# Cross-attention on one core: which engine issues the first two moves of a quad's probabilities, and what SyncE issues ahead of the slot's loads

## The chip, the core and the metric

The kernel runs on one core of one Trainium2 chip. The metric is the device time of one execution in microseconds; the median of 3 runs before is 567.95 us (567.91 to 568.03). Short names of the engines, as the profile has them: PE is TensorE (PEld its weight loads), DVE is VectorE, ACT is ScalarE, POOL is GpSimd, SP is SyncE. SPq and ACTq are the queues from which SyncE and ScalarE issue DMAs.

## The reference

Layer norm of x, a query projection, attention of 32 heads of width 32 over a context that is both keys and values, an output projection and a residual:

```python
# x, ctx_4096: (8, 256, 1024) float32; the mask is all ones; Wq, Wout: (1024, 1024)
mu = jnp.mean(hidden_states, axis=-1, keepdims=True)
var = jnp.var(hidden_states, axis=-1, keepdims=True)
x = (hidden_states - mu) * jax.lax.rsqrt(var + LN_EPS) * ln_gamma + ln_beta
Q = _split_heads(x @ Wq.T)
K = _split_heads(memory_keys)
V = _split_heads(memory_values)
scores = jnp.einsum('bhsd,bhtd->bhst', Q, K) * scale
scores = jnp.where(mask, scores, -jnp.inf)
probs = jax.nn.softmax(scores, axis=-1)
attn = jnp.einsum('bhst,bhtd->bhsd', probs, V)
attn = attn.transpose(0, 2, 1, 3).reshape(B, S, HIDDEN)
out = attn @ Wout.T
return residual + out
```

## The kernel before

All data is float32. The work is cut into 64 quads: quad n is four heads (index j, 0 to 3) of batch n // 8, so eight quads make a batch. An outer loop over slots, n = 0 to 63, writes every engine's instructions in a fixed order by hand (`tc.manual_schedule()`); engines run their own streams in order and meet at semaphores. Slot n holds, on PE, the scores of quad n + 1 (`scores`, L486), the product of probabilities and values of quad n - 2 (`values`, L636), and pieces of the query projection of a later batch (L447) and of the output projection of the batch before (L720). From batch 2 on, both projections go by a scheme of seven half-size products; weights for it are kept in DRAM and read back through a tile `ring` (L412).

`softmax_parts(n)` writes the softmax of one quad. For each head and each half of the 256 queries DVE adds the mask bias and takes the row minimum of the negated scores (L524, with a read of its accumulator, `mn`), and ACT takes the exponential and its row sum (L528, `den`). DVE inverts the sums (L535, `rden`), POOL multiplies (L543; in some quads DVE or ACT does a head), and DVE transposes 32 x 32 blocks of each head into a tile `pT` (`blocks`, L549). The scores lie in four PSUM buffers, one per head, that the next quad's scores overwrite: PE can start the next scores only when DVE has read these.

A 32 x 32 block transpose does not carry blocks across partitions. The rest is done by moving quarters of 32 partitions. `pT` has two halves (index 0 and 1) on the second dimension. ACT copies aside the second half into a tile `pc` (`aside`, L555), two heads at a time, the second time behind the last block transpose. Then `tail` issues four DMAs of 128 KB each:

- the first two moves (L614): first half of partition group 2r + 1 to the second half of group 2r, for r = 0 and 1; they overwrite what `aside` read, so they wait for it;
- the second two moves (L618): from `pc`, group 2r, to the first half of group 2r + 1; they overwrite what the first moves read, so each waits for a first move's landing.

Between the first two and the second two SP issues the loads of the slot (`between`): keys for quads n + 4 and n + 5 (L135, `load_k`) or values for two later quads (L143, `load_v`), and in some slots residual rows `r` (L149), half of a later x (L129), a mask, halves of `ring` (L412). Loads in `ahead` stand ahead of all four moves. After the tail, in some slots, ACT normalizes half of an x (L248), DVE takes its statistics (L227) or transposes it (L316), SP issues four or six moves of x (`move_x`, L332), and results are sent out (L763).

For quads 0 to 7 and 57 to 63 the tail is put off into the next quad's softmax (`tails`); for quads 8 to 56 it stands at the end of the quad's own softmax. There the next thing on ACT behind the second copy aside is, but for a normalization of x in some slots, the next quad's first exponential. Tiles rotate: three buffers for `pT` and for `pc`, two for keys and for values, four for `r`.

Of the kernel before, what the change touches and what calls it, by code (L numbers as in the profile page):

```python
# [59 lines left out]
def xattn_kernel(  # L60
# [10 lines left out]
    nc = tc.nc  # L71
# [4 lines left out]
    NQ = NC  # L76
# [4 lines left out]
    K = 32  # L81
# [4 lines left out]
    N = B * NQ  # L86
# [404 lines left out]
    def softmax(*args):  # L491
        for _ in softmax_parts(*args):
            pass
# [2 lines left out]
    BY_ACT = range(1, 2 * NQ)  # L496
    BY_DVE = range(NQ, 2 * NQ)


    def softmax_parts(n, copies=(), ahead=(), between=(), hooks={}, fill=()):  # L500

        fill = list(fill)

        def fill_in():
            if fill:
                fill.pop(0)()  # L510

        pss = scs[n]
        pT = pTs[n] = ptp.tile([P, 2, NI, NH, NS, K], F32, tag="pT", name=f"pT_{n}")
        pc = asp.tile([P, NI, NH, NS, K], F32, tag="pc", name=f"pc_{n}")
        es, mns, dens = {}, {}, {}

        def exps(j, part=range(NS)):
            if 0 in part:
                es[j] = ep.tile([P, NS, T], F32, tag="e", name=f"e_{n}_{j}")
                mns[j] = sm.tile([P, NS], F32, tag="mn", name=f"mn_{n}_{j}")  # L520
                dens[j] = sm.tile([P, NS], F32, tag="den", name=f"den_{n}_{j}")
            e, mn, den = es[j], mns[j], dens[j]
            for s in part:
                nc.vector.tensor_tensor_reduce(  # L524
                    out=e[:, s, :], in0=pss[j][:, s, :], in1=mbs[n // NQ], scale=1.0,
                    scalar=NO_SCORE, op0=ALU.add, op1=ALU.min, accum_out=mn[:, s : s + 1],
                )
                nc.scalar.activation(  # L528
                    e[:, s, :], e[:, s, :], AF.Exp, bias=mn[:, s : s + 1], scale=-1.0,
                    accum_out=den[:, s : s + 1],  # L530
                )

        def normalize(j):
            rden = sm.tile([P, NS], F32, tag="rden", name=f"rden_{n}_{j}")
            nc.vector.reciprocal(rden, dens[j])  # L535
            for s in range(NS):
                if j == NH - 1 and n in BY_ACT:
                    nc.scalar.activation(
                        es[j][:, s, :], es[j][:, s, :], AF.Copy, scale=rden[:, s : s + 1]
                    )  # L540
                    continue
                engine = nc.vector if j == 1 and n in BY_DVE else nc.gpsimd
                engine.tensor_scalar(  # L543
                    es[j][:, s, :], es[j][:, s, :], rden[:, s : s + 1], 1.0,
                    ALU.mult, ALU.mult,
                )

        def blocks(j):
            nc.vector.transpose(  # L549
                pT[:, :, :, j, :, :].rearrange("p a i s k -> p (a i) s k"),  # L550
                es[j].rearrange("p s (b t) -> p b s t", t=K),
            )

        def aside(j):
            nc.scalar.copy(pc[:, :, ts(j, 2)], pT[:, 1, :, ts(j, 2)])  # L555

        if n == 0:
            for j in range(NH - 1):
                exps(j, (0,))
            yield  # L560
            exps(NH - 1, (0,))
            fill_in()
            yield
            for j in range(NH):
                exps(j, (1,))
            normalize(0)
            fill_in()
        else:
            exps(0)
            while tails:  # L570
                tails.pop()()
            for done in list(pvs):
                copy_at(done)
            exps(1)
            for hook in hooks.get("soon", ()):
                hook()
            exps(2)
            normalize(0)
            exps(3)
        if n <= NQ + 1:  # L580
            for copy in copies:
                copy()
        for hook in hooks.get(0, ()):
            hook()
        normalize(1)
        fill_in()
        if n in BY_DVE:
            normalize(2)
        blocks(0)
        for hook in hooks.get(1, ()):  # L590
            hook()
        if n not in BY_DVE:
            normalize(2)
        fill_in()
        if n in BY_ACT:
            normalize(3)
        blocks(1)
        aside(0)
        if n not in BY_ACT:
            normalize(3)  # L600
        fill_in()
        blocks(2)
        while fill:
            fill_in()
        if n > NQ + 1:
            for copy in copies:
                copy()

        def tail():
            blocks(3)  # L610
            aside(1)

            for r in range(2):
                nc.sync.dma_start(pT[ts(2 * r, K), 1], pT[ts(2 * r + 1, K), 0])  # L614
            for load in between:
                load()
            for r in range(2):
                nc.sync.dma_start(pT[ts(2 * r + 1, K), 0], pc[ts(2 * r, K)])  # L618

        for load in ahead:  # L620
            load()
        if n < NQ or n > N - NQ:
            tails.append(tail)
        else:
            tail()
        yield
# [16 lines left out]
    def copy_at(n):  # L643
        b, c = divmod(n, NQ)
        k, c = divmod(c, NK)
        if c == 0:
            ats[b, k] = atp.tile([P, NK, NS, NA, K], F32, tag="at", name=f"at_{b}_{k}")
        for r, pv in enumerate(pvs.pop(n)):
            nc.scalar.copy(
                ats[b, k][:, c, :, ts(r, 2), :], pv.rearrange("p a s k -> p s a k")  # L650
            )
# [245 lines left out]
    for c in range(NC):  # L897
        copy_x0(1, c, nc.scalar if c < NC // 2 else nc.vector)
    first = softmax_parts(0, (partial(copy_q, 1), partial(copy_q, 2)), (), (), {}, [
        partial(ln_stats, 1, 0), partial(ln_stats, 1, 1),  # L900
        partial(ln_norm, 1, 0, nc.vector),
# [17 lines left out]
    for b in range(B - 1):  # L919
        done, ends = 0, b == B - 2  # L920
        for i, counts in enumerate(steps_of(b)):
            n = NQ * (b + 1) + i
# [15 lines left out]
    for n in range(N):  # L938
        b, i = divmod(n - NQ, NQ)
        new_q = new_qs[n]  # L940
        between = []
# [5 lines left out]
        if n + 3 in firsts or n + 2 in firsts:  # L947
            between, ahead = between + ahead, []
# [214 lines left out]
```

## Time and profile before

| | |
|---|---|
| median of 3 runs | 567.95 us (567.91 to 568.03) |
| profiled execution, from its first to its last instruction (span) | 566.0 us |
| what lies around the span, against the median | 1.95 us |
| PE, DVE, ACT, POOL busy | 561.4, 467.6, 423.4, 394.3 us |
| granted clock of PE over the span | 1.000 |
| bytes moved by DMA, mean rate | 119.02 MB, 210 GB/s |

No time of the profiled execution other than its span is given, so the span stands for it. Busy times are sums over the span; matmuls are pipelined and their ends are modelled. A row of a group reads: line, engine, operation, tile written, tile read, shapes, count, then busy us and mean ns. A row of the timeline reads: start in us, duration in us, engine, line, operation, tiles, count, and in brackets the idle time of the engine before it and what ended it. A row of waits reads: engine, line and what it waited for, then us in total, times, longest us. A row of one line's instructions reads: minimum, median and maximum duration in ns, and when the first and the last start.

### The profile page before, as it was taken

How to read it: one execution, taken by the hardware profiler on the slowest of the kernel's cores; microseconds unless marked ns; L12 is line 12 of the kernel's file. 1: busy time of each engine (PE TensorE's matmuls, PEld its weight loads, DVE VectorE, ACT ScalarE, POOL GpSimd, SP SyncE). 2: the span in 40 equal slices, each digit the busy share in tenths (PEclk: the TensorE clock that was granted, in tenths of full speed). 3: DMA queues.
4: the chain of work that ended last, by engine and by line, in shares of the span. 5: the costliest groups of instructions: out<-in, count | busy, mean ns of one | idle time of the engine just before them, and what ended most of it. 6: DMA issues, size and time to landing. Idle time of an engine off the chain costs nothing.

```text
span 566.0 us, 20200 instructions
## 1 busy us (share of the span) xinstructions
PE 561.4 (99%) x7266; PEld 393.7 (70%) x7266; DVE 467.6 (83%) x1716; ACT 423.4 (75%) x1464; POOL 394.3 (70%) x636
## 2 busy tenths in 40 slices
PE   8999999999999999999999999999999999999997
PEld 8788886767766767667766776667766767755454
DVE  5889889999988988878898888988888777879923
ACT  4699999997778866786777876778776776769820
POOL 2788887899777656857568665777648657448780
PEclk9999999999999999999999999999999999999999
DMA  8966667856697777966778767796658864536751
GB/s 310 397 181 199 185 198 228 281 162 179 212 301 232 223 202 235 263 195 191 233 216 239 215 176 221 230 273 193 176 140 269 255 191 128 146 110 180 218 156 74
DMA packets 47219, 119.02 MB, mean 210 GB/s; under 512 B 8976, under 2 KB 9744, under 8 KB 47120
## 3 DMA queue, kind: packets, MB, share of 16 engines
q1 hardware_dynamic: 46976, 117.74, 69.5%
q8 instruction: 57, 0.93, 0.8%
q14 instruction: 42, 0.34, 0.2%
q10 hardware_dynamic: 144, 0.01, 0.0%
HBM read 66.33 MB, written 11.53 MB: 138 GB/s over the span
## 4 chain that ended last, share of the span: by engine, by line
PE 97%; DMA 1%; DVE 0%; POOL 0%; ACT 0%; issue 0%; SPq 0%; POOLq 0%
PE po_S L720 21%; PE pq_A L447 19%; PE pv L636 12%; PE sc L486 12%; PE po_A L720 11%; PE pq L345 9%; PE pq_S L447 8%; PE po_end L787 3%; PE po_last L787 1%; DMA x<-in_x_dram 1%; PE po_end_s L787 0%; POOL x L885 0%; PE pq L290 0%; PE px L307 0%; ACT e L528 0%; PE px L273 0%
## 5 line engine op out<-in xcount | busy, mean ns | idle before, releaser
L543 POOL TENSOR_SCALAR e<-e,rden 128x256 f32<-128x256 f32 x466 | 215.4, 479 | 125.5 <-DVE rden L535 123.0
L528 ACT ACTIVATE e<-e,mn 128x256 f32<-128x256 f32 x512 | 254.0, 502 | 46.1 <-DVE mn L524 44.9
L549 DVE STREAM_TRANSPOSE pT<-e 128x512 f32<-128x512 f32 x256 | 178.9, 703 | 35.6 <-POOL e L543 27.5
L524 DVE CUSTOM_DVE_ANT_0 e<-sc,mb 128x256 f32<-128x256 f32 x512 | 185.3, 415 | 25.4 <-PE sc L486 25.1
L555 ACT COPY pc<-pT 128x512 f32<-128x512 f32 x128 | 79.0, 617 | 55.7 <-DVE pT L549 35.6
L528 ACT ACTIVATION_READ_ACCUMULATOR e<-e,mn 128x1 f32 x512 | 98.4, 192 | 0.0
L486 PEld LDWEIGHTS sc<-k,qa 32*128 32x128 f32 x1024 | 46.1, 184 | 42.2 <-issue 21.6
L720 PE MATMUL po_S<-wo,at 128*128 128x512 f32 x152 | 74.3, 606 | 0.0
L636 PE MATMUL pv<-pT,v 64*32 64x128 f32 x4096 | 74.1, 274 | 0.0
L486 PE MATMUL sc<-k,qa 32*128 32x256 f32 x1024 | 73.6, 401 | 0.1
L636 PEld LDWEIGHTS pv<-pT,v 64*32 64x32 f32 x4096 | 57.0, 105 | 22.5 <-issue 11.8
L720 PE MATMUL po_A<-wo,at 128*128 128x512 f32 x128 | 59.4, 605 | 0.0
L345 PE MATMUL pq<-xnT,wq 128*128 128x256 f32 (+1 forms) x240 | 55.0, 384 | 0.0
L447 PEld LDWEIGHTS pq_A<-xnT,wq 128*128 128x128 f32 x416 | 48.5, 192 | 6.2 <-issue 4.8
L345 PEld LDWEIGHTS pq<-xnT,wq 128*128 128x128 f32 x240 | 44.6, 190 | 8.2 <-issue 1.5
L720 PE MATMUL po_S<-wo,s 128*128 128x512 f32 x104 | 50.1, 606 | 0.0
L447 PE MATMUL pq_A<-xnT,wq 128*128 128x128 f32 x416 | 48.5, 275 | 0.0
L535 DVE RECIPROCAL rden<-den 128x2 f32<-128x2 f32 x256 | 38.2, 150 | 7.3 <-ACT e L528 6.2
L524 DVE DVE_READ_ACCUMULATOR2_ANT mn<- 128x1 f32 x512 | 42.4, 83 | 0.0
L720 PEld LDWEIGHTS po_A<-wo,at 128*128 128x128 f32 x128 | 22.9, 189 | 25.6 <-issue 24.5
L720 PEld LDWEIGHTS po_S<-wo,at 128*128 128x128 f32 x152 | 25.5, 190 | 19.5 <-issue 19.5
L753 POOL TENSOR_TENSOR r<-r,p 128x512 f32<-128x512 f32 x24 | 30.6, 1277 | 4.8 <-ACT e L528 3.0
(102 smaller groups left out, 666.1 us busy)
## 6 DMA issues: line engine op xcount, KB each, us to landing
v<-in_kv_dram SPq DMA_DIRECT2D x32, 512.0 KB, 4.2
pT<-pT SPq DMA_DIRECT2D x128, 128.0 KB, 2.9
pT<-pc SPq DMA_DIRECT2D x128, 128.0 KB, 4.0
ring<-kept_T SPq DMA_DIRECT2D x20, 512.0 KB, 5.3
k<-in_kv_dram SPq DMA_DIRECT2D x32, 256.0 KB, 4.1
x<-in_x_dram SPq DMA_DIRECT2D x15, 512.0 KB, 5.6
r<-in_x_dram SPq DMA_DIRECT2D x28, 256.0 KB, 4.5
out_dram<-r SPq DMA_DIRECT2D x28, 256.0 KB, 3.2
```

What stands on the lines that cost most here:

```text
L345: nc.tensor.matmul(pqs[n], wq[:, o, c, :], xnTs[b](c), start=(c == 0), stop=(c == NC - 1),)
L447: nc.tensor.matmul(pqs[b][:, o, :], w[:, c], x_[:, c], start=begins and o + c == 0, stop=c == NK - 1, skip_group_check=True,)
L486: nc.tensor.matmul(scs[n][j][:, s, :], qa[r, n % NQ, ts(s, P)], ks[n - n % 2][r, n % 2, :], start=True, stop=True,)
L524: nc.vector.tensor_tensor_reduce(out=e[:, s, :], in0=pss[j][:, s, :], in1=mbs[n // NQ], scale=1.0, scalar=NO_SCORE, op0=ALU.add, op1=ALU.m ...
L528: nc.scalar.activation(e[:, s, :], e[:, s, :], AF.Exp, bias=mn[:, s : s + 1], scale=-1.0, accum_out=den[:, s : s + 1],)
L535: nc.vector.reciprocal(rden, dens[j])
L543: engine.tensor_scalar(es[j][:, s, :], es[j][:, s, :], rden[:, s : s + 1], 1.0, ALU.mult, ALU.mult,)
L549: nc.vector.transpose(pT[:, :, :, j, :, :].rearrange("p a i s k -> p (a i) s k"), es[j].rearrange("p s (b t) -> p b s t", t=K),)
L555: nc.scalar.copy(pc[:, :, ts(j, 2)], pT[:, 1, :, ts(j, 2)])
L636: nc.tensor.matmul(pvs[n][r][j * HD : (j + 1) * HD], vs[n - n % 2][ts(r, 2 * K), i, ds(n % 2 * P + j * HD, HD)], pT[ts(r, 2 * K), :, i, j, ...
L720: nc.tensor.matmul(po, operand(b, name)[:, c], wo[:, which, c], start=begins and c == 0, stop=c == NK - 1, skip_group_check=not begins,)
L753: nc.gpsimd.tensor_tensor(r, r, p1s[b], ALU.add)
```

## The change

In quads 14 to 55 (`SOONER`) the first two moves are issued from ACT's queue instead of SP's, directly behind the second copy aside. On SP the second two moves go ahead of the loads of `between` instead of behind them. All other quads are as before; the copies, moves, loads and their bytes are the same.

```diff
     BY_DVE = range(NQ, 2 * NQ)
+
+    SOONER = range(2 * NQ - 2, N - NQ)
...
             blocks(3)
             aside(1)
 
+            queue = nc.scalar if n in SOONER else nc.sync
             for r in range(2):
-                nc.sync.dma_start(pT[ts(2 * r, K), 1], pT[ts(2 * r + 1, K), 0])
-            for load in between:
-                load()
+                queue.dma_start(pT[ts(2 * r, K), 1], pT[ts(2 * r + 1, K), 0])
+            if n not in SOONER:
+                for load in between:
+                    load()
             for r in range(2):
                 nc.sync.dma_start(pT[ts(2 * r + 1, K), 0], pc[ts(2 * r, K)])
+            if n in SOONER:
+                for load in between:
+                    load()
```

## The prediction

> **What bounds the kernel now.** I read the page first: span, busy shares, chain that ended last.
>
> ```profile
> span 566.0 us, 20200 instructions
> PE 561.4 (99%) x7266; PEld 393.7 (70%) x7266; DVE 467.6 (83%) x1716; ACT 423.4 (75%) x1464; POOL 394.3 (70%) x636
> PE 97%; DMA 1%; DVE 0%; POOL 0%; ACT 0%; issue 0%; SPq 0%; POOLq 0%
> ```
>
> TensorE (PE) is busy for 561.4 of 566.0 us and carries 97% of the chain. An average hides stages, so next comes the busy time by engine in two stretches of eight quads each (one batch), both inside the quads that the change touches.
>
> ```profile
> core 0: us, PE busy (x) PEld busy (x) DVE busy (x) ACT busy (x) POOL busy (x), PEclk, DMA share, GB/s
> 155.80:223.80 68.00, 68.00 (x922) 48.12 (x922) 58.27 (x213) 51.32 (x180) 46.00 (x81) 1.00 0.79 233
> 291.90:359.70 67.80, 67.80 (x922) 47.91 (x921) 57.96 (x213) 51.27 (x180) 45.86 (x81) 1.00 0.74 208
> ```
>
> PE is busy for the whole of each stretch, at full granted clock: nothing in quads 14 to 55 makes it wait, so work of other engines there can only be hidden or become a new stall. ScalarE (ACT) has 67.8 - 51.3 = 16.5 us of idle time per batch. What of it is free shows in ACT's waits, by stretch (third: 223.9 to 291.8 us, fourth: 359.8 to 427.7 us).
>
> ```profile
> ACT pc L555 <- DVE pT L549: 6.4, 7, 1.6
> ACT e L528 <- DVE mn L524: 5.8, 5, 1.4
> ACT pc L555 <- DVE rden L535: 4.6, 7, 1.9
> ...
> ACT e L528 <- DVE mn L524: 6.3, 6, 1.4
> ACT pc L555 <- DVE pT L549: 6.2, 6, 1.6
> ACT pc L555 <- DVE rden L535: 3.9, 7, 0.8
> ...
> ACT e L528 <- DVE mn L524: 5.4, 5, 1.4
> ```
>
> The first three rows are the stretch from 155.8 us; the next three hold, in equal figures, for the stretches from 223.9 and from 291.9 us; the last is the fourth. Two of the waits are in the middle of a quad: both copies aside (L555) wait for VectorE's (DVE's) block transposes, behind ScalarE's own exponentials and GpSimd's (POOL's) normalization. They move with the exponentials and cover nothing. Only "e <- mn" lies where the new issues go, between a quad's last copy aside and the next quad's first exponential: 5.8, 6.3, 6.3 and 5.4 us, mean 6.0 us per batch.
>
> One such place, in order of time, at quad 34's end and quad 35's start:
>
> ```profile
> 300.64 0.62 ACT L555 COPY pc<-pT 128x512 f32<-128x512 f32 x1 [1.01 <-DVE pT L549]
> 300.68 1.15 PE L486 MATMUL sc<-k,qa 32*128 32x256 f32 x16
> 301.29 1.14 SPq L614 DMA_DIRECT2D pT<-pT  x2
> 302.13 0.41 DVE L524 CUSTOM_DVE_ANT_0 e<-sc,mb 128x256 f32<-128x256 f32 x1
> 302.46 0.08 DVE L524 DVE_READ_ACCUMULATOR2_ANT mn<- 128x1 f32 x1
> 302.64 0.51 ACT L528 ACTIVATE e<-e,mn 128x256 f32<-128x256 f32 x1 [1.38 <-DVE mn L524]
> 303.55 0.18 ACT L528 ACTIVATION_READ_ACCUMULATOR e<-e,mn 128x1 f32 x1
> 304.19 0.16 DVE L535 RECIPROCAL rden<-den 128x2 f32<-128x2 f32 x1
> 304.59 0.42 DVE L524 CUSTOM_DVE_ANT_0 e<-sc,mb 128x256 f32<-128x256 f32 x1
> 309.19 1.15 PE L486 MATMUL sc<-k,qa 32*128 32x256 f32 x16
> 319.63 1.16 PE L636 MATMUL pv<-pT,v 64*32 64x128 f32 x64
> ```
>
> Scores of quad 35 start at 300.68; DVE's eighth and last read of them ends at 304.59 + 0.42 = 305.01; PE overwrites their buffers at 309.19. So the softmax may fall 4.2 us behind PE before PE stops: that is the cover. At the other end, quad 34's probabilities are used at 319.63, while their moves are issued here from 301.29: landing sooner is worth nothing.
>
> **The two issues on ScalarE.** Work, bytes and tiles stay; per touched quad two DMA issues leave SyncE's (SP's) queue and enter ScalarE's, behind the second copy aside and ahead of all that the next quad does there.
>
> ```profile
> L614 SPq DMA_DIRECT2D pT<-pT x128: 507/582/2155, 26.0 to 540.8; - x128
> L193 ACTq DMA_DIRECT2D gb<-in_gamma_beta_dram x1: 377/377/377, 1.0 to 1.0; - x1
> pT<-pT SPq DMA_DIRECT2D x128, 128.0 KB, 2.9
> pT<-pc SPq DMA_DIRECT2D x128, 128.0 KB, 4.0
> x<-in_x_dram SPq DMA_DIRECT2D x15, 512.0 KB, 5.6
> k<-in_kv_dram SPq DMA_DIRECT2D x32, 256.0 KB, 4.1
> ```
>
> An issue of exactly this move holds SP's queue for 0.582 us (median of 128, least 0.507). The only issue on ScalarE in this trace, of another shape, took 0.377. Because the move overwrites what the copy reads, it must wait for the copy's end: SP's issue starts 0.03 us behind it (300.64 + 0.62 = 301.26, then 301.29). Meanwhile no exponential can overtake it on ScalarE. The first exponential then starts about 0.10 us after its releaser (302.46 + 0.08 = 302.54, then 302.64). The gap between copy and exponential is therefore p = 0.03 + 2 x 0.582 + 0.10 = 1.29 us. Lower bound: two of ScalarE's own issue and nothing for the restart, 0.03 + 2 x 0.377 = 0.79. Two of SP's fastest give 1.04. Upper bound: SP's pairs of moves sometimes take longer; I take half an issue more, 1.6. I take 1.29, the row of the same move.
>
> The chain this lengthens runs in a ring: second copy aside, issues, exponentials of the next quad, reciprocal, normalization on POOL, block transpose, second copy aside. Per batch it gains 8 x 1.29 = 10.3 us and has 6.0 us free: 4.3 us over. In 42 touched quads, 5.25 batches, that is 22.7 us; the first 4.2 us of the lag are hidden by the distance to PE's overwrite, and from there on PE waits for DVE's reads: 22.7 - 4.2 = 18.5 us.
>
> **What else moves.** I collect it in q, us per batch.
> - Relief: the reciprocal of a quad's first head starts at 304.19, behind DVE's sixth read, though its denominator is ready at 303.55 + 0.18 = 303.73. With ScalarE late and DVE waiting, that 0.46 goes; the later heads then wait for their own exponentials, so I count 0.2 per quad, 1.6 per batch.
> - The slot's loads go from ahead of SP's second moves to behind them, and these wait for the first moves' landing. So loads start some 0.03 + 2.9 + 2 x 0.58 - 1.19 = 2.9 us later. Keys and values are needed slots later. Residual r(0,0) is nearer: issued at 297.35 now, landing 5.4 later at 302.75, used by POOL at 302.86. Some 2.9 late, less the lag already there, it costs 0 to 1 us per batch; I take 0.6.
>
> ```profile
> 297.35 0.43 SPq L149 DMA_DIRECT2D r<-in_x_dram  x1
> DMA to landing us min/median/max: 5.4/5.4/5.4
> 302.86 1.27 POOL L753 TENSOR_TENSOR r<-r,p 128x512 f32<-128x512 f32 x1
> 311.15 0.59 SPq L135 DMA_DIRECT2D k<-in_kv_dram  x1
> 341.14 5.18 SPq L332 DMA_DIRECT2D xnT<-xe  x6
> ```
>
> - The built program gives its DMAs eight completion counters in turn, and an issue first waits until the counter's last DMA has landed. On SP that wait held only SP; now it holds the exponentials. Mostly that DMA is long done, but at quads 15, 24, 32 and 40 ScalarE's second move stands eight behind a 512 KB load of x. From the copy aside of the quad before, that load lands after a first and a second move's issue (0.03 + 1.16), 2.9 of landing, SP's two second moves (1.16, priced as first ones), k (0.59) and 5.6 of its own: 11.4 us, or 10.9 if SP's first of them starts as the first move lands. ScalarE's second move is ready after one quad of 8.5 us and 0.6: it waits some 1.8 us, once a batch, of which DVE's extra work in that quad hides part; I take 1.0 (0 to 2).
>
> Relief and costs cancel: q = 0, from -1.6 to +3. The sum is 567.95 + 5.25 x (8p - 6.0 + q) - 4.2, never below 567.95: 586.4 us. Against the profiled execution: its span of 566.0 lies 1.95 under the median, and I expect a span of 584.4. Least difference that a measurement of this kernel can tell from none: about 0.2%, 1.1 us.
>
> **The rivals.**
> - Hidden, no change: 567.95 us. It needs 8p + q - 6.0 under 4.2 / 5.25 = 0.8, which with q = 0 is p under 0.85 us. For it: 0.79 from ScalarE's own issue. Against it: that is a fetch of other shape, and p must also hold the wait and the restart. The Trainium skill ("DMA: Bandwidth & Descriptors", section "Issuing engines are not separate DMA queues") says that the time to initiate a DMA is usually small relative to the DMA itself; by that rule it would be this rival. The rows here have 0.582 beside 2.9 to landing, a fifth, on an engine whose chain is nearly full.
> - Faster, because probabilities land sooner. PE waits for none: 18 us lie between first issue and use, and PE's stretches have no idle time. It could give at most what is outside them, and those stages are untouched. I give 2%; its time would be under 566.8.
> - Heavier: ScalarE's issues queue with SP's. In three quads of a batch SP issues four to six moves of x just then (5.18 us for six, in the last row above). If each of ScalarE's six issues there waits for half of a 0.58 us issue, q rises by 6 x 0.29 = 1.7; with the counters' waits in full, q = +3 and the time is 586.4 + 15.8 = 602. The Trainium skill ("Perfetto Trace Analysis", section "DMA Instruction — HWDGE (DVE, Sync)") has a lock wait in each issue, for a generator that two issuing sequencers share; it would be this rival, and no trace here shows two engines issuing at once.
> - Light: p near 1.04 with the relief in full, 5.25 x (8.3 - 6.0 - 1.6) - 4.2 = 0 to 8 us, 569 to 574.
>
> That the change does not do what it says is out: the built program has 84 of these moves in ScalarE's stream, each pair directly behind the second copy aside.
>
> **How the numbers follow.** Forecast, 574 to 597 us (p of 1.04 to 1.55 with q near 0): 62%. Heavier, 597 to 606: 12%. Light, 569.1 to 574: 12%. Hidden: 12%. Faster: 2%. So slower 86%, same 12%, faster 2%. The range from 570 to 602 leaves out hidden, faster and the far ends of light and heavy, about 2 in 10. The likeliest case gives 586.4.
>
> **What would show it.** Right: two issues on ACT's queue of about 0.58 us behind each copy aside of quads 14 to 55; "e <- mn" gone from ACT's waits there; PE's scores waiting for DVE's reads, so that PE's slots, equal from batch to batch now (67.9 us), grow to about 71 to 72 from the second touched batch on while the first is still mostly covered; DVE's reciprocals released by ACT. The counters' wait would show as an issue on ACT's queue that starts over 1 us behind its copy aside at quads 15, 24, 32 and 40. Wrong: PE still busy for the whole of these stretches, with ACT's gap under 0.85 us or DVE's and POOL's part of the ring shrinking by over 0.5 us per quad.

## The result and the profile after

The changed kernel takes 597.11 us (median of 4 runs, 594.06 to 600.01); the kernel before took 567.99 us (567.91 to 568.03) beside it. The ratio is 1.0509, 95% interval 1.0481 to 1.0536: 29 us slower. In the first three experiments below one run of four took over 1.5% longer than the fastest run of its kernel, and it is left out of their medians, ranges and ratios. The profiled execution took 597.22 us, its span 595.4. The span, the busy times and the chain of the page after:

```profile
span 595.4 us, 20171 instructions
PE 571.1 (96%) x7266; PEld 395.8 (66%) x7266; DVE 472.9 (79%) x1716; ACT 424.4 (71%) x1464; POOL 394.6 (66%) x636
DMA 21%; PE 19%; ACT 16%; POOL 15%; DVE 15%; issue 7%; ACTq 4%; SPq 3%; DVEq 0%; POOLq 0%
```

PE carried 97% of the chain before and carries 19% now; the chain runs through every engine and through DMAs. The span grew by 29.4 us: PE sits idle for 24.3 us (595.4 - 571.1) where it was idle for 4.6, and its busy time, for the same 7266 matmuls, grew by 9.7 us. The waits of the kernel after (engine, line, what it waited for, then us in total, times, longest):

```profile
DVE rden L537 <- ACT e L530: 47.7, 55, 2.2
...
PE po_S L727 <- DVE r L769: 15.7, 12, 2.2
...
ACT e L530 <- DMA pT<-pT: 11.4, 4, 3.3
...
POOL r L760 <- DMA r<-in_x_dram: 7.2, 3, 3.8
```

DVE's reciprocals now wait for ScalarE's exponentials (47.7 us; 6.2 before). PE waits for one thing above all (15.7 us in 12 waits), and it is not the scores: it is the output projection's one PSUM buffer, `po`, which DVE must add into `r` before PE may write it again.

The timeline shows one whole stall, at quad 38's end and quad 39's start. First ScalarE, then DVE, then PE, of the kernel after:

```profile
353.64 0.62 ACT L557 COPY pc<-pT 128x512 f32<-128x512 f32 x1 [1.55 <-DVE pT L551]
354.29 2.10 ACTq L617 DMA_DIRECT2D pT<-pT  x2
356.49 0.51 ACT L530 ACTIVATE e<-e,mn 128x256 f32<-128x256 f32 x1 [2.23 <-DMA pT<-pc]
...
357.61 0.17 DVE L537 RECIPROCAL rden<-den 128x2 f32<-128x2 f32 x1 [1.96 <-ACT e L530]
...
358.43 0.69 DVE L769 TENSOR_TENSOR r<-po_S,r 128x512 f32<-128x512 f32 x1
...
353.10 3.84 PE L447 MATMUL pq_A<-sx,ring 128*128 128x128 f32 x32
359.17 2.07 PE L727 MATMUL po_S<-wo,s 128*128 128x512 f32 x2 [2.23 <-DVE r L769]
```

The two issues hold ScalarE from 354.29 to 356.39; the exponential starts 2.23 us behind the copy; DVE, in order, stands at the reciprocal for 1.96 us; the add of `po` into `r` is queued behind that reciprocal; PE, whose order is fixed as well, waits 2.23 us. This is not a plain hold: the second issue starts 0.67 us later than in a plain quad and takes 0.87 us where a plain one takes 0.60, so the two last 2.10 us and not 1.16. The same place before, DVE and then PE:

```profile
339.56 0.69 DVE L762 TENSOR_TENSOR r<-po_S,r 128x512 f32<-128x512 f32 x1
...
337.73 3.84 PE L447 MATMUL pq_A<-sx,ring 128*128 128x128 f32 x32
341.41 1.88 PE L720 MATMUL po_S<-wo,s 128*128 128x512 f32 x4
```

There the add ended at 340.25 and PE came to the buffer at 341.41: 1.2 us of cover, where the prediction had counted 4.2 for the scores.

The prediction's first sign did show: the two issues stand behind each copy aside. At a plain quad the gap is the predicted 1.29 us, as ScalarE's timeline after shows at quad 37's end:

```profile
345.15 0.62 ACT L557 COPY pc<-pT 128x512 f32<-128x512 f32 x1 [0.23 <-DVE pT L551]
345.81 1.16 ACTq L617 DMA_DIRECT2D pT<-pT  x2
347.07 0.51 ACT L530 ACTIVATE e<-e,mn 128x256 f32<-128x256 f32 x1 [1.29 <-DVE mn L526]
```

The bracket names `mn`, but DVE had read it by 346.57, and the issues end at 346.97. The profile puts such a gap down to a semaphore all the same, so the sign that `e <- mn` would be gone from ACT's waits can't be read from its waits, which still have 44.5 us of them (44.9 before).

### The profile page after: what moved, and what is told of

It reads as the page before. It is cut to its first block, busy times and chain, and to the rows that moved or that the text cites. A ratio compares the mean times of both kernels' runs of the same rounds, so it can differ in the third digit from the quotient of the medians.

```text
span 595.4 us, 20171 instructions
## 1 busy us (share of the span) xinstructions
PE 571.1 (96%) x7266; PEld 395.8 (66%) x7266; DVE 472.9 (79%) x1716; ACT 424.4 (71%) x1464; POOL 394.6 (66%) x636
## 4 chain that ended last, share of the span: by engine, by line
DMA 21%; PE 19%; ACT 16%; POOL 15%; DVE 15%; issue 7%; ACTq 4%; SPq 3%; DVEq 0%; POOLq 0%
POOL e L545 12%; ACT e L530 9%; DMA pT<-pT 9%; DVE pT L551 7%; DMA r<-in_x_dram 4%; PE po_S L727 4%; DMA x<-in_x_dram 4%; ACTq L617 4%; ACT pc L557 3%; PE po_A L727 3%; DVE e L526 3%; PE po_end L794 3%; PE pv L643 2%; PE sc L486 2%; PE pq_A L447 2%
## 5 line engine op out<-in xcount | busy, mean ns | idle before, releaser
L530 ACT ACTIVATE e<-e,mn 128x256 f32<-128x256 f32 x512 | 253.9, 501 | 66.7 <-DVE mn L526 44.5
L727 PE MATMUL po_S<-wo,at 128*128 128x512 f32 x152 | 76.0, 618 | 5.2 <-DVE r L769 4.1
L537 DVE RECIPROCAL rden<-den 128x2 f32<-128x2 f32 x256 | 39.2, 154 | 48.9 <-ACT e L530 47.7
L486 PE MATMUL sc<-k,qa 32*128 32x256 f32 x1024 | 75.5, 406 | 0.3 <-DVE qa L468 0.2
L727 PE MATMUL po_S<-wo,s 128*128 128x512 f32 x104 | 52.7, 632 | 11.6 <-DVE r L769 11.6
L727 PEld LDWEIGHTS po_A<-wo,at 128*128 128x128 f32 x128 | 22.9, 189 | 26.1 <-issue 24.5
L727 PEld LDWEIGHTS po_S<-wo,s 128*128 128x128 f32 x104 | 18.4, 196 | 29.8 <-issue 16.3
```

Source lines behind the costliest of these rows:

```text
L486: nc.tensor.matmul(scs[n][j][:, s, :], qa[r, n % NQ, ts(s, P)], ks[n - n % 2][r, n % 2, :], start=True, stop=True,)
L530: nc.scalar.activation(e[:, s, :], e[:, s, :], AF.Exp, bias=mn[:, s : s + 1], scale=-1.0, accum_out=den[:, s : s + 1],)
L727: nc.tensor.matmul(po, operand(b, name)[:, c], wo[:, which, c], start=begins and c == 0, stop=c == NK - 1, skip_group_check=not begins,)
```

## The experiments

Each kernel was timed beside the kernel before; "+x us" is the difference of the medians of that comparison. To place a loss I use the pitch of a quad: the start of the next quad's first score matmul on PE minus the start of its own. The table holds, for the profiled executions, the growth of the pitch against before, summed over quads 12 to 59 by quad number modulo 8 (us). One profiled execution can differ by some us from the median; that of the order alone took 613.53 us.

```
quad modulo 8          0     1     2     3     4     5     6     7   sum
the change           7.9   0.9   0.4   7.9   0.1   1.6   0.0  10.0  28.7
issue alone          6.2   0.0   7.5   8.9   0.4   0.9   0.0   5.7  29.7
order alone          0.0   0.5   0.0  44.4   0.0   0.0   0.0  -0.1  44.9
order, r put back    0.0   0.0   0.0  30.3   0.0   0.0   0.0   0.0  30.3
bare hold, 1.26 us   2.6   0.0   0.0   1.8   0.0   0.3   0.0   5.9  10.5
quads 1 to 6 only    1.5   0.0   0.0  15.8   0.0   0.1   0.0   7.7  25.1
 the same, r back    0.9   0.0   0.0   8.1   0.0   0.2   0.0   5.8  15.0
quads 7 and 0 only   1.6   0.1   0.7   0.0   0.0   0.0   0.0   0.1   2.5
quads 2, 4, 6 only   1.1   0.0   0.0   4.8   0.0   0.2   0.0   0.1   6.2
change, r put back   5.7   0.0   1.8  17.9   0.0   0.0   0.0   3.3  28.8
 and x moved         8.2   0.0   1.2  12.2   0.0   0.4   0.0   5.9  27.9
```

**The two parts alone.** First the issue on ScalarE without the new order of loads:

```diff
-                nc.sync.dma_start(pT[ts(2 * r, K), 1], pT[ts(2 * r + 1, K), 0])
+                queue.dma_start(pT[ts(2 * r, K), 1], pT[ts(2 * r + 1, K), 0])
```

> The change without its second part: ScalarE issues the first two moves, but the slot's loads stay ahead of SyncE's second moves, as in the kernel before. Theory A (the gap of 1.29 us that two issues make on ScalarE between a quad's last copy aside and the next quad's first exponential is the main cost): the ledger 8 x 1.29 - 6.0 = 4.3 us per batch stays, the late residual rows and most of the waits for a landed counter go, the relief of up to 1.6 remains: 5.25 x (4.3 - 0.8) less 1 us of cover is 17 us over before, 585 us, bounds 578 to 592. Rival B (the loads behind the second moves, late by 3 us or more, are the main cost): at most 574 us.

Measured: 597.89 us (595.29 to 598.11), ratio 1.0491 (1.0450 to 1.0532), +29.0 us: over the range of A, and far over that of B. Then the new order without the issue (`queue = nc.sync` in the change):

> The second part alone: SyncE issues all four moves, second moves ahead of the slot's loads, in quads 14 to 55. Theory A: ScalarE's gap is as before (0 to 1.4 us, with DVE as the releaser), only residual rows come some 3 us late once a batch and may use up the 1 us of cover there: 568 to 571 us. Rival B: over 585 us.

Measured: 605.94 us (605.83 to 613.53), ratio 1.0697 (1.0624 to 1.0770), +37.1 us: as B had it, and A is wrong. One move on each queue, with the new order (`queue = nc.scalar if n in SOONER and r == 0 else nc.sync`):

> As the change, but ScalarE issues only one of the two first moves and SyncE the other. Theory A: the gap on ScalarE falls from 1.29 to 0.03 + 0.52 + 0.10 + 0.1 = 0.7 to 0.75 us; 8 x 0.75 = 6.0 is just what was free per batch, so nearly all is hidden, but for the quads without a free place and the late residual rows: 568 to 574 us. Rival B: the loads are as late as in the change, so over 585 us. Rival C (what costs is the wait of the issue for the copy's end and the restart, not the time of the issues): over 585 us too.

Measured: 603.51 us (600.23 to 604.44), ratio 1.0597 (1.0555 to 1.0639), +34.7 us: A is wrong again, and this time alone does not tell B from C; no line of its trace is used here.

The issue alone shows neither wait for r nor for the ring. There PE waits for the output projection's buffers (13.5 us for `po` and 5.3 for the buffer that it shares with the query projection), and ScalarE's mean gap is 2.00 us against 1.78 in the change: with the loads ahead, the counters hold the first move too. ScalarE's timeline of that kernel at quad 32's end:

```profile
299.97 0.62 ACT L557 COPY pc<-pT 128x512 f32<-128x512 f32 x1 [0.42 <-DVE pT L551]
303.54 1.19 ACTq L617 DMA_DIRECT2D pT<-pT  x2
304.83 0.51 ACT L530 ACTIVATE e<-e,mn 128x256 f32<-128x256 f32 x1 [4.24 <-issue]
```

Each part alone costs as much as both or more, so they do not add. The order part, which the prediction had priced at 0 to 1 us a batch, is the dearer one (37 us by the medians, 40 by the ratio). The waits of the order-alone kernel:

```profile
POOL r L760 <- DMA r<-in_x_dram: 41.8, 5, 9.4
DVE r L769 <- POOL r L760: 37.9, 6, 8.6
...
PE pq_S L447 <- DMA ring<-kept_T: 24.3, 5, 5.8
```

GpSimd waits five times, once a batch, for the residual r(0,0), and PE itself five times for the second half of the ring's T1; PE waits for values too, twice, for 4.1 us. All but 0.5 us of the loss lies in quads 3 modulo 8, where r(0,0) and T1 are used.

**The hold alone.** No DMA changes its queue or its place; ScalarE copies something once more behind the second copy aside, in the same quads. SyncE's first moves wait for that copy too, and the loads behind them with it:

```diff
             aside(1)
+            if n in SOONER:
+                nc.scalar.copy(pc, pT[:, 1])
+                nc.scalar.copy(pc[:, 0, 0], pT[:, 1, 0, 0])   # second kernel only
```

> No DMA is moved or reordered: the kernel before, with one more copy on ScalarE behind the second copy aside of quads 14 to 55, which writes the same 1024 values per partition to the same tile once more (as long as an activation of 128 x 1024, 1.25 us, of which 1.15 us keep the next instruction away). Theory A: 8 x 1.15 - 6.0 = 3.2 us per batch, less a relief of up to 1.6, times 5.25, less 1 us of cover: 576 to 584 us, with SyncE's first moves 1.15 us later at no cost. Rivals B and C: 568 us.

> The hold of the last call made longer: behind the second copy aside in quads 14 to 55 ScalarE does a copy of 128x1024 and one of 128x64 more; no DMA is moved, SP issues all as before. The gap between copy aside and next exponential should be 1.27 us, that of the change, up from about 1.13. S: the gap alone makes the loss, so about the time of the change: 590 to 600. Ledger: 4 us of the last call plus 5.25 x 8 x 0.14 = 6: 574 to 580. W agrees with the ledger here, and lays the other 20 us to waits that only issues have.

The one copy makes a gap of 0.98 us in a plain quad (not the 1.13 that the later expectation names) and falls between its two expectations: 572.09 us (571.75 to 572.87), ratio 1.0060 (1.0040 to 1.0080), +3.2 us. The two make 1.26 us and cost 579.62 us (579.38 to 580.0), ratio 1.0189 (1.0169 to 1.0209), +10.9 us. From the second kernel, ScalarE's timeline and one of the waits:

```profile
336.85 0.62 ACT L556 COPY pc<-pT 128x512 f32<-128x512 f32 x1 [0.23 <-DVE pT L550]
337.50 1.05 ACT L614 COPY pc<-pT 128x1024 f32<-128x1024 f32 x1
338.58 0.24 ACT L615 COPY pc<-pT 128x64 f32<-128x64 f32 x1
338.73 0.50 ACT L529 ACTIVATE e<-e,mn 128x256 f32<-128x256 f32 x1
```

```profile
PE po_S L724 <- DVE r L766: 5.6, 8, 1.2
```

Hence a hold as long as the plain gap of the change (1.26 of 1.29 us) stalls PE at the same buffer and costs 11 of the 29 us. SyncE's first moves start 1.38 us behind the copy aside at a plain quad of this run, and 0.03 us in the change; still, PE waits for no ring here, and GpSimd 0.8 us for r. Between the two holds, 0.28 us more in 42 quads, 11.8 us in all, came out as 7.6 us: about 0.64 us for each us that ScalarE is held, once the free time is used up. The rival that the gap alone makes the loss (590 to 600) is wrong. The ledger by batches (574 to 580) gave the right range by luck: it took 0.14 us for the step between the two holds, which is 0.28, and full price for each us held. With 0.28 it would have said 584.

**Which quads.** The change in some quads only:

```diff
-    SOONER = range(2 * NQ - 2, N - NQ)
+    SOONER = [n for n in range(2 * NQ - 2, N - NQ) if n % NQ in range(1, NQ - 1)]
```

> The change as it is, but only in quads 17 to 54 whose number modulo 8 is 1 to 6 (31 of the 42; quad 14 too). The other 11 (numbers 7 and 0 modulo 8, where loads and moves of x stand in SP's queue) are as before. S, steady: the loss is 29 us by 42 equal quads, 0.69 us each, from the gap of 1.29 us on ScalarE. Then 31 quads cost 21 us: 587 to 591. W, waits: the gap costs what the bare hold of the last call cost, about 4 us, and the rest is in the quads where ScalarE's issue waits for a completion counter behind x or is a long one. Then 571 to 577.

Measured: 593.24 us (592.16 to 595.16), ratio 1.0431 (1.0403 to 1.0460), +24.5 us, over both ranges. With `n % NQ in (NQ - 1, 0)`:

> The complement of the one before: the change only in the 11 quads whose number modulo 8 is 7 or 0. S: 11 x 0.69 = 7.6 us, 574 to 577. W: most of the loss, 580 to 592. If the two complements do not add up to 29 us (both under 577), the loss needs both together: waits that cost because the steady gap has used up the free time before them.

Measured: 570.73 us (570.26 to 572.55), ratio 1.0037 (1.0023 to 1.0052), +2.0 us, under both ranges. With `n % NQ in (2, 4, 6)`:

> The change only in quads whose number modulo 8 is 2, 4 or 6: 16 quads, 3 in a batch, none next to another. The prediction's ledger by batches: 3 x 1.29 = 3.9 us of gap against 6.0 free: nothing, 567.5 to 569.5. S, every quad for itself: 16 x 0.69 = 11 us, 577 to 581. In between if free time cannot be carried from quad to quad: half of the gap's excess over 0.75 us a quad, 16 x 0.54 = 9 at most, less the cover.

Measured: 572.17 us (568.93 to 574.16), ratio 1.0050 (1.0031 to 1.0069), +3.4 us.

The complements nearly add up (26.5 of 29.1), and the 11 quads with the waits behind x cost little by themselves: W falls. But S falls too: the table has 15.8 of the 25.1 us of the 31 quads in quads 3 modulo 8, where the bare hold has 1.8. What stands there is again loads behind SyncE's second moves: GpSimd waits 14.5 us for r in three waits and PE 6.6 us for the ring in three. One of them, in a line of GpSimd's timeline of the run with quads 1 to 6:

```profile
174.39 1.26 POOL L760 TENSOR_TENSOR r<-r,p 128x512 f32<-128x512 f32 x1 [5.57 <-DMA r<-in_x_dram]
```

The three quads a batch land between their two expectations. 3 x 1.29 us of hold does fit into the free time (nothing shows in quads 7); most of what is left lies in quads 3 modulo 8, 4.8 of 6.2 us in the profiled execution, where GpSimd again waits for r (12.3 us in four waits over the span).

**Putting loads back.** In the next four the residuals `r` go ahead of SyncE's second moves again, as before the change; in one of them, the loads of x go ahead of all four moves too. The edit against the change is, but for those two parts (x, and which quads):

```diff
-            if n not in SOONER:
-                for load in between:
-                    load()
+            for load in between:
+                if n not in SOONER or load.func is load_res:
+                    load()
...
-            if n in SOONER:
-                for load in between:
-                    load()
+            for load in between:
+                if n in SOONER and load.func is not load_res:
+                    load()
```

> The order part alone (SyncE issues all four moves, second moves ahead of the loads), but the residuals r stay ahead of the second moves. R: the whole 41 us of the order part was one load a batch, r(0,0): 568 to 571. Rival: keys, values, ring and x behind the second moves cost as well; then over 575.

Order alone with r back: 598.11 us (595.57 to 599.96), ratio 1.0525 (1.0495 to 1.0555), +30.1 us. R expected none of the loss to stay; 7 of 37 us went by the medians (10 of 40 by the ratios) and 30 stayed, as the rival had it. The ring's half had stood behind r, and is late by itself. SyncE's queue, then PE, then the waits of this kernel:

```profile
310.17 1.15 SPq L617 DMA_DIRECT2D pT<-pT  x2
311.36 0.59 SPq L149 DMA_DIRECT2D r<-in_x_dram  x1
315.64 2.02 SPq L622 DMA_DIRECT2D pT<-pc  x2
317.71 0.57 SPq L135 DMA_DIRECT2D k<-in_kv_dram  x1
318.34 0.43 SPq L412 DMA_DIRECT2D ring<-kept_T  x1
...
316.14 1.95 PE L447 MATMUL pq_S<-sx,ring 128*128 128x128 f32 x16
323.49 1.86 PE L447 MATMUL pq_S<-sx,ring 128*128 128x128 f32 x7 [5.40 <-DMA ring<-kept_T]
...
PE pq_S L447 <- DMA ring<-kept_T: 20.2, 5, 5.4
POOL r L760 <- DMA r<-in_x_dram: 4.2, 3, 2.0
```

SyncE can issue nothing between 311.95 and 315.64, because the second moves at the head of its queue wait for the first moves' landing; they take 2.02 us, and the ring's load is issued at 318.34. The product has 32 matmuls in the trace; the first 16 use the first half of the ring and end at 318.09, so PE already stands before the second half when its load goes out. Before the change the same load went out ahead of the second moves (SyncE's queue, PE from its 17th matmul of the product on, and the load's size and time to landing in that window):

```profile
296.86 0.45 SPq L412 DMA_DIRECT2D ring<-kept_T  x1
...
305.59 1.95 PE L447 MATMUL pq_S<-sx,ring 128*128 128x128 f32 x16
...
ring<-kept_T SPq DMA_DIRECT2D x1, 512.0 KB, 4.8
```

It landed at 296.86 + 4.8 = 301.7, and the matmuls that use this half began at 305.59: 3.9 us of cover, about the landing of one first move (median 3.6 us in this run, 4.2 in the change).

> The change as it is, but the loads of residuals r stay where they were, ahead of SyncE's second moves; all other loads go behind them as in the change. R, three costs: the hold of 1.29 us on ScalarE (about 10 us, in the slots whose quad is 7, 0 and 3 modulo 8), the residual r(0,0) that lands late (about 6 us, in quads 3 modulo 8), and ScalarE's issues waiting for counters and queue (about 12 us, in quads 7 and 0 modulo 8). Then only the second goes: 589 to 593. G, the gap alone with little cover: nothing changes, 595 to 599.

The change with r back: 596.75 us (593.09 to 597.8), ratio 1.0493 (1.0459 to 1.0526), +28.7 us. R is wrong; G has the time, though not for its reason, since the bare hold had shown that the gap alone makes 11 us. GpSimd's wait for r is gone from the waits, and PE's wait for the ring took its place (1.7 us in two waits with the change as it is):

```profile
PE pq_S L447 <- DMA ring<-kept_T: 12.4, 5, 3.9
PE po_S L727 <- DVE r L769: 6.1, 6, 1.8
```

> The change in all 42 quads, residuals r ahead of the second moves, and the load of a half of x, where a slot has one, ahead of that quad's four moves. That shifts the eight counters: what stands eight behind ScalarE's second move at quads 24, 32 and 40 is no longer the 512 KB load of x but a 64 KB move, and x itself is issued some 6 us earlier. R: against the run with only r put back, the second move's wait at quads 24, 32 and 40 (2.6 to 3.3 us gaps) falls to under 1 us and 5 to 9 us come back: 580 to 586. If that wait is not what costs, as with r put back: 589 to 593.

With x moved as well: 598.08 us (594.51 to 599.63), ratio 1.0519 (1.0478 to 1.0559), +30.1 us, over both ranges. The wait that it aimed at did shrink; ScalarE's queue at quad 24's end, with r back and then with x moved too:

```profile
226.85 3.57 ACTq L617 DMA_DIRECT2D pT<-pT  x2
```

```profile
229.68 1.38 ACTq L617 DMA_DIRECT2D pT<-pT  x2
```

Nothing came back all the same: outside the quads that normalize x, gaps over 2.5 us stand at quads 15, 16, 22, 23 and 39 instead, and PE waits for `po` for 10.9 us and for the ring for 9.1. So this run does not settle what the counters' waits are worth: they moved to other quads, and ScalarE's mean gap stayed (1.84 against 1.82 us).

> The change in the quads 1 to 6 modulo 8 only (31 of 42), with the residuals r ahead of the second moves. R: neither late r nor waits for counters behind x are left, only the hold in 31 quads: 574 to 579, its loss in the quads 7 and 0 modulo 8, nothing above 2 us in quads 3 modulo 8. Rival: late values or rings take the place of r: over 583.

The quads 1 to 6 with r back: 584.7 us (582.08 to 589.74), ratio 1.0315 (1.0254 to 1.0375), +16.7 us. Here putting r back did return 7.8 us, but not down to the hold: quads 3 modulo 8 still hold 8.1 us, and PE waits 4.9 us in three waits for the ring. The rival for this run, late rings in the place of r (over 583), holds.

## Why the prediction was right, and where it was off

The sign and the range held; the point lay 10.7 us low. That the range held is in part luck. The hold, which the forecast made the whole loss, was priced at 18.5 us, and a bare hold of nearly its length costs 10.9; the other costs, netted to nothing, came to 18.2. The two errors offset in part, and 597.1 lies at the upper end of the forecast, where the range of the heavier rival begins.

- **PE bounds, nothing to gain: right.** No run came out faster than before.
- **The gap p = 1.29 us: right to the hundredth** at a plain quad, and by its parts: the two issues hold ScalarE for 1.16 us (0.51 and 0.60 with 0.04 between them), and the exponential starts 0.10 us behind them.
- **The ring and its 6.0 us of free time a batch: right in kind, too dear.** With 1.26 us for p, the formula without q says 17.2 us; the bare hold of 1.26 us cost 10.9. The relief of 1.6 us a batch that the prediction put into q belongs here: with it the formula says 8.8. It does not fit both holds, though: for 0.98 us it says nothing with the relief, and 3.2 us were measured. DVE's waits for ScalarE, 6.2 to 47.7 us, show that DVE did come to stand behind it.
- **The cover: the wrong buffer.** The prediction took the scores' buffers (4.2 us). PE's score matmuls wait 0.2 us in all; PE stops at `po`, whose add sits on DVE behind the reciprocals, with 1.2 us of cover at the place shown. So the sign that the first touched batch would be mostly covered failed: from the scores of quad 16 to those of quad 24 it took 74.0 us, 6.0 more than before the change, and the later ones took 72.0 to 74.8 where 71 to 72 was forecast. It looked only at what PE overwrites of the quad's own and not at other work queued on DVE behind the delayed instruction.
- **q = 0: the term that was mis-sized.** Relief taken out, q stood for 1.6 us a batch of costs, 8.4 us over 5.25 batches. The change costs 29.1 us and the bare hold 10.9, so they came to 18.2 us, 3.5 a batch. Two parts of it were named and one was missed. *Residual r(0,0), 0 to 1 us a batch:* 7.2 us of waits in the change, but up to 9.4 us at one time where SyncE issues all moves. *Counters:* the second move starts 1.4 to 2.1 us late at quads 15, 24, 32 and 40, as named; the mean gap in the 42 quads is 1.78 us against 1.50 with the bare hold, some 12 us more of ScalarE's time, which at 0.64 would be worth 7 to 8 us. Of the 12, 7.6 us are second moves that start late and 3.1 longer issues. What this is worth to PE is worked out and not shown: the run made to show it moved the waits only. *The ring's half:* "keys and values are needed slots later" passed over the load in `between` that PE needs soonest, with 3.9 us of cover.
- **Why the parts do not add.** With SyncE issuing all four moves in the new order, it falls behind: the first moves start up to 6.6 us behind their copy aside (quads 31 to 34 of the order alone with r back), against 0.03 us when ScalarE issues them. With ScalarE issuing, GpSimd waits 7.2 us for r and not 41.8, and PE 1.7 us for the ring and not 24.3. So it seems that ScalarE's issue pays back most of what the new order costs in late loads, and pays for it with the hold and the counters' waits.
- **Rivals.** Hidden, light and faster are out. The rule that the time to initiate a DMA is usually small relative to the DMA itself (the Trainium skill, "DMA: Bandwidth & Descriptors", "Issuing engines are not separate DMA queues") agrees with these rows for the transfer (0.58 us beside 4.2 to landing), but it does not make the issues free: a hold as long as two of them, in 42 quads, is worth 11 us of the kernel. Heavier, by queueing of ScalarE's issues with SyncE's, is there in kind and small: the 84 issues take 50.1 us, 1.2 more than 84 of 0.582, though one takes 2.19. Its other part, the counters' waits, came at 1.4 to 2.1 us where 1.8 was worked out.

What stays open is how the 18 us beyond the hold divide between counters, r and ring within the change itself. By the table, the change loses 6.1 us more than the bare hold in quads 3 modulo 8, where r and ring are used, 9.4 more in quads 7 and 0, and 2.7 in the others; that places the time and does not prove its cause. Each try to take one cause away gave its time to another.

## What to carry to other kernels

A DMA issue on a compute engine is an instruction of that engine: price it by what is queued behind it, follow that to the next engine's in-order queue, and look there for the work of other stages, which may have less cover (1.2 us here against 4.2). When an issue that waits for a landing is moved ahead of loads, every load behind it starts a landing later; list them by who awaits each, and begin with the one that the bounding engine reads. Where several waits have little cover (here 0.1 us for r, 1.2 for `po`, 3.9 for the ring), removing one can show nothing; take the parts alone, and a bare hold of equal length beside them, before laying the loss to any of them.

## What the runs showed of the hardware

A pause of PE can cost more than its length. PE's timeline after, and then the same scores before:

```profile
149.96 2.83 PE L727 MATMUL po_S<-wo,at 128*128 128x512 f32 x4 [1.93 <-DVE r L769]
152.72 1.66 PE L486 MATMUL sc<-k,qa 32*128 32x256 f32 x12
```

```profile
146.93 1.88 PE L720 MATMUL po_S<-wo,at 128*128 128x512 f32 x4
148.74 1.15 PE L486 MATMUL sc<-k,qa 32*128 32x256 f32 x16
```

Behind a pause of 1.93 us four matmuls took 2.83 us and not 1.88, and the scores after them ran at 0.14 us each and not 0.07. The granted clock (PEclk) behind this pause, behind one of 1.70 us that ends at 223.55, and behind the one of 2.23 us at quad 39, after:

```profile
core 0: us, PE busy (x) PEld busy (x) DVE busy (x) ACT busy (x) POOL busy (x), PEclk, DMA share, GB/s
151.00:154.00 3.00, 3.00 (x15) 1.34 (x17) 2.74 (x5) 1.89 (x6) 2.13 (x3) 0.50 0.86 272
221.00:227.00 6.00, 4.30 (x60) 2.51 (x61) 4.83 (x14) 5.14 (x18) 3.59 (x8) 1.00 0.74 210
359.20:362.50 3.30, 3.30 (x4) 1.48 (x5) 2.90 (x7) 2.27 (x9) 3.10 (x7) 0.50 0.63 140
```

The Trainium skill ("TensorE: Matmul & The Clock Gate", "What's actually happening") has the array fall to half its clock after at least one idle window of about 3.4 us. The halving agrees with these rows, the length does not: a pause of 1.93 us sufficed here, and one of 1.76 us in the issue-alone run (at 162.47). Nor does the length alone decide it: behind a pause of 2.37 us in the run with x moved (at 176.71) the clock stayed at 1.00.

In the kernel after, the clock was halved twice in the middle of the span, for 3.4 us each time by the trace, which at half the clock makes 3.4 us of lost time. That is only a part of the 9.7 us by which PE's busy time grew. In the run with the bare hold of 1.26 us it grew by 5.8 us (567.2 against 561.4) at a granted clock of 1.00, so the rest has another cause, which stays open; the ends of matmuls are modelled.

The same 128 KB moves take another time to land. The issues of the kernel after (size, median us to landing), and then those of the order-alone kernel:

```profile
pT<-pc SPq DMA_DIRECT2D x128, 128.0 KB, 2.4
pT<-pT ACTq DMA_DIRECT2D x84, 128.0 KB, 4.2
```

```profile
pT<-pT SPq DMA_DIRECT2D x128, 128.0 KB, 4.0
```

The first moves land in 4.2 us (2.9 before), and in 4.0 where SyncE issues them in the new order; the second moves went from 4.0 to 2.4. So it is not the issuing queue. In both orders the slower moves are those issued next behind a slot's loads: before the change the second moves of the same quad, in the new order the first moves of the next. That it is the loads' traffic that slows them fits these medians and was not tested. The longer landing lengthens the second moves' wait for the first, and with it every load's.
